# Attention outputs of the second pass by two levels of seven products, with weight sums prepared in the first pass

## The chip, the cores and the metric

The kernel runs on one core of one Trainium2 chip. The metric is the device time of one execution in microseconds. The engines are called as in the profile: PE is TensorE (PEld its weight loads), DVE is VectorE, ACT is ScalarE, POOL is GpSimd, and SP issues nearly all the DMA transfers.

## What is computed

The reference is a block of four layers over x (8 sequences of 256 rows, 1024 wide, fp32): an autocorrelation layer with a context, a linear layer with low-rank experts, an attention over the context, and a linear layer with a Fourier-transformed update. Each is added to x with a gate. The change touches the third, whose reference is, cut down:

```python
q = rope(query @ wq)            # 32 heads of 128
k, v = rope(key @ wk), value @ wv   # 8 heads; 4 query heads share one
p = softmax(mask(q @ k.T))
out = concat_heads(p @ v) @ wo  # (256 x 4096) @ (4096 x 1024)
x = x + tanh(g_xattn[1]) * out
```

Everything is fp32.

## The kernel before

**Passes and blocks.** The eight sequences are done in two passes (`p` = 0, 1) of four. A pass keeps its rows of x in SBUF (`xt`, eight tiles of 128 rows) and runs the four layers one after the other: `autocorrelation` with `keys_values` beside it, `lora_ffn`, `attention`, `fourier_ffn`. Within attention there are 16 steps `(blk, g)`: two blocks of 512 rows, and for each the eight groups of four query heads that share a key head.

**Seven products instead of eight.** Matrix products are done by one level of the Strassen-Winograd scheme: both operands are cut into 2 x 2 quarters, seven products of sums of quarters are made, in the order `SEVEN = (1, 2, 6, 7, 4, 5, 3)`, and their results are added up on eviction from PSUM. `left_operands` and `right_operands` (lines 203 and 212) make the operands with four additions each. `combine` (220) adds the products of queries, keys and values; `add_product` (252) adds those of the outputs into x, with the gate. The operand sums of wq and wo are made once, in the first block of the first pass, written to DRAM (`wq_d`, `wo_d`) and loaded from there later (`load_wq` 862, `load_wo` 884); a step loads seven tiles of 512 KB of each.

**What a step puts on the engines.** `queries` (921) makes the queries of the next step, 7 products of 8 matmuls of 128x256, evicted by VectorE and ScalarE, and rotated by `rope` (714): three VectorE multiplications and one GpSimd addition. `scores` (969) does four matmuls of 128x256 for each pair of heads, into two PSUM tiles; VectorE copies them under the mask into tiles that GpSimd has filled with a large negative number (985), and a softmax by VectorE and ScalarE follows. `values` (1006) transposes the weights on TensorE and multiplies them by v. `outputs` (942) multiplies the attention of the step before by wo: 7 products, each for two tiles of 128 rows, with two matmuls of 128x512 for a tile.

**The order** is written out by hand with generators. Each step has four quarters `i`, one for each `(n, l)`: scores, then `q_fill[i]` query products, then output products by `o_fill[i]`, in the midst of the `values` of the quarter before. The Tile framework issues the instructions of each engine from that order, as operands and buffers come free in its own planning. PSUM tiles: four of `ps_mm` (queries and outputs), two of `ps_sc` (scores), two of `ps_wa` (transposed weights and values). In SBUF the big tiles are in three groups of seven of 4 KB a partition: the tags a and b hold weights, "xn" holds operands of x.

Of the kernel before, what the change touches and what calls it, by code (L numbers as in the profile page):

```python
# [11 lines left out]
F32 = mybir.dt.float32  # L12
# [7 lines left out]
P = 128  # L20
# [26 lines left out]
def flamingo_kernel(ctx: ExitStack, tc: tile.TileContext, a: dict, out: bass.AP):  # L47
# [25 lines left out]

    tab = const.tile([P, 2, S], F32, name="tab")
    tab_q = const.tile([P, 2, S], F32, name="tab_q")
# [3 lines left out]
    def load_constants():  # L79
        nc.sync.dma_start(tab, a["rope"])  # L80
        nc.sync.dma_start(tab_q, a["rope_q"])
        nc.sync.dma_start(rows, a["rows"])
        nc.sync.dma_start(gates[:, :, 0], a["g_xattn"].partition_broadcast(P))
        nc.sync.dma_start(gates[:, :, 1], a["g_ffn"].partition_broadcast(P))
        nc.scalar.activation(tg, gates, AF.Tanh)
        nc.vector.tensor_scalar(ntg, tg, -1.0, None, ALU.mult)
        nc.sync.dma_start(gate_b, a["gate_b"].partition_broadcast(P))
# [12 lines left out]
        [dram.tile([P, 2, HALF], F32, name=f"wo_d{g}_{i}") for i in range(4)] for g in range(N_KV)  # L100
    ]

    wk_d, wv_d = (
# [115 lines left out]

    def combine(r, ps, tiles, new, dest):  # L220


        if r == 1:
            tiles["u"] = new("u")
            nc.scalar.copy(tiles["u"], ps)
        elif r == 2:
            c = dest()
            nc.vector.tensor_add(c, ps, tiles["u"])
            return c, (0, 0)
        elif r == 6:  # L230
            nc.vector.tensor_add(tiles["u"], ps, tiles["u"])
        elif r == 7:
            tiles["w"] = new("w")
            nc.vector.tensor_add(tiles["w"], ps, tiles["u"])
        elif r == 5:
            m = new("m")
            nc.scalar.copy(m, ps)
            nc.gpsimd.tensor_add(tiles["u"], tiles["u"], m)
            c = dest()
            nc.gpsimd.tensor_add(c, tiles["w"], m)  # L240
            return c, (1, 1)
        elif r == 3:
            c = dest()
            nc.vector.tensor_add(c, ps, tiles["u"])
            return c, (0, 1)
        elif r == 4:
            c = dest()
            nc.vector.tensor_sub(c, tiles["w"], ps)
            return c, (1, 0)
        return None  # L250
# [462 lines left out]

    def rope(dst, ps, cos, sin, pool):

        H = P // 2
        t0 = pool.tile([P, 2, S], F32, tag="rope0", name="rope0", bufs=1)
        t1 = pool.tile([P, 2, S], F32, tag="rope1", name="rope1", bufs=1)
        tab = lambda t: t.unsqueeze(1).to_broadcast([t.shape[0], 2, S])
        nc.vector.tensor_mul(t0, ps, tab(cos))  # L720
        nc.vector.tensor_mul(t1[0:H], ps[H:P], tab(sin[H:P, :]))
        nc.vector.tensor_mul(t1[H:P], ps[0:H], tab(sin[0:H, :]))  # L722
        nc.gpsimd.tensor_add(dst, t0, t1)  # L723

    def keys_values(n, groups, pools):

# [60 lines left out]
        for u in range(4):  # L787
# [4 lines left out]
            for r in SEVEN:  # L792
# [14 lines left out]
                out_tile = lambda: w2.tile([P, 2, S], F32, tag="kv", name=kind[1])  # L807
                dest = (lambda: new("c")) if kind == "wk" else out_tile
                done = combine(r, ps, tiles, new, dest)
                if done:  # L810
                    c, (i, j) = done
                    if kind == "wk":
                        kT = out_tile()
                        rope(kT, c, tab[:, 0, :], tab[:, 1, :], w1)
                        place = kT_d.rearrange("(q l i) p t -> q i p l t", l=2, i=2)
                        nc.sync.dma_start(
                            place[i_u, i, :, :, t0 + j * S : t0 + (j + 1) * S], kT
                        )
# [11 lines left out]

    def query_operands(xt, norm, pool, ps_t, tag):

# [3 lines left out]
        for t in range(NBT):  # L836
            xn = pool.tile([P, D], F32, tag="xn", name="xl")
            normed(xn, xt[t], mv, rstd, t)
# [6 lines left out]
        s = [big_tile("xn", [KH, S], f"xn_t{i}") for i in (1, 2, 4)]  # L845
        return right_operands(nc.vector, q, *s)

    def attention(p, xt, gq, go, keep, norms, xops):
        with (
# [6 lines left out]
            steps = [(blk, g) for blk in range(TT // NBT) for g in range(N_KV)]  # L859
            wq, wo, kv = {}, {}, {}  # L860

            def load_wq(step):
# [21 lines left out]
            def load_wo(step):  # L884
# [12 lines left out]
                else:  # L897
                    ops = {}
                    where = {1: a["wo"][g, 0, 0], 2: a["wo"][g, 1, 0], 3: a["wo"][g, 1, 1]}
                    where |= dict(zip((5, 7, 6, 4), wo_d[g]))  # L900
                    for r in SEVEN:
                        ops[r] = big_tile(go, [2, HALF], f"wo_{r}")
                        nc.sync.dma_start(ops[r], where[r])
                wo[step] = ops

            def load_kv(step):
                blk, g = step
                r0 = p * BP * S + blk * NB
                kT = w2.tile([P, NB], F32, tag="kv", name="kT", bufs=4)
                nc.sync.dma_start(kT, kT_d[g, :, r0 : r0 + NB])  # L910
                v = w2.tile([P, NBT, DH], F32, tag="kv", name="v", bufs=4)
                nc.sync.dma_start(
# [8 lines left out]
            def queries(step, qT):  # L921
# [3 lines left out]
                for r in SEVEN:  # L925
                    ps = ps_mm.tile([P, 2, S], F32, tag="mm", name="ps_q")
                    for l in range(2):
                        for c in range(KH):
# [6 lines left out]
                            )  # L935
                    done = combine(r, ps, tiles, lambda tag: half(tag, 1), lambda: half("c", 2))
                    if done:
                        qT[done[1]] = half("qT", 8)
                        rope(qT[done[1]], done[0], tab_q[:, 0, :], tab_q[:, 1, :], w1)
                    yield  # L940

            def outputs(step, ops):
# [11 lines left out]
                for r in SEVEN:  # L954
                    for t in range(2):
# [9 lines left out]
                        flat = [y.rearrange("p b s -> p (b s)") for y in part[t]]  # L965
                        add_product(r, po, x[t], tg_x[1], ntg_x[1], flat)
                    yield

# [37 lines left out]
            def values(step, l, n, got, oT, fill):  # L1006
# [14 lines left out]
                for i in range(2):  # L1021
                    for c in range(2):
# [6 lines left out]
                        )  # L1029
                oT[n][l] = half("oT", 8)  # L1030
                nc.scalar.copy(oT[n][l], av)

            def fill_from(gen, n):
                for _ in range(n):
                    next(gen, None)

            load_wq(steps[0])
            load_kv(steps[0])
# [4 lines left out]
            load_wq(steps[1])  # L1043
            last, before, nothing = None, None, iter(())

            q_fill = {0: (2, 2, 1, 1), len(steps) - 1: (0, 0, 0, 0)}
            o_fill = {len(steps) - 1: (2, 2, 2, 1)}
            oT = [[None, None], [None, None]]
            for k, step in enumerate(steps):
# [7 lines left out]
                else:  # L1057
                    q_gen = nothing
                o_gen = nothing
                for i, (n, l) in enumerate(((0, 0), (0, 1), (1, 0), (1, 1))):  # L1060
                    got = scores(step, l, n, qT)
                    nq = q_fill.get(k, (3, 3, 1, 0))[i]
                    no = o_fill.get(k, (0, 1, 3, 3))[i]
                    fill_from(q_gen, nq)
                    if i > 0:
                        fill_from(o_gen, no - 1)
                    if before is not None:
                        values(*before, lambda: fill_from(o_gen, 1 if no else 0))
                    before = step, l, n, got, oT
                    if i == 0 and k > 0:  # L1070
                        s = [half(f"oS{j}", 1) for j in (1, 2, 4)]
                        o_gen = outputs(last[0], left_operands(nc.gpsimd, last[1], *s))
                        fill_from(o_gen, no)
                    if i == 2 and k + 2 < len(steps):
                        if steps[k + 2][1] == 0:
                            blk = steps[k + 2][0]
                            xb = xt[blk * NBT : (blk + 1) * NBT]
                            xops[blk] = query_operands(xb, norms[blk], w1, ps_wa, "wa")
                        load_wq(steps[k + 2])
                    if i == 0:  # L1080
                        load_wo(step)
                for gen in (q_gen, o_gen):
                    for _ in gen:
                        pass
                last = step, oT
                oT = [[None, None], [None, None]]
                qT = following
            values(*before, lambda: None)
            s = [half(f"oS{j}", 1) for j in (1, 2, 4)]
            for _ in outputs(last[0], left_operands(nc.gpsimd, last[1], *s)):  # L1090
                pass
# [66 lines left out]
    for p in range(NPASS):  # L1158
        ga, gb = ("a", "b") if p % 2 == 0 else ("b", "a")
        xt = [xpool.tile([P, D], F32, tag="x", name="x") for t in range(TT)]  # L1160
        with (
# [9 lines left out]
        ):  # L1171

            def beside():
                for n in range(p * BP * S // NB, (p + 1) * BP * S // NB):
                    yield from keys_values(n, (ga, gb), (kw1, kw2, ps_kv))
                if p == 0:
# [7 lines left out]
            steps = beside()  # L1184
            next(steps)
            if p == 0:
                load_constants()
# [10 lines left out]
        with tc.tile_pool(name="at_keep", bufs=1, reuse_waits="tile") as kp:  # L1198
            keep, norms, xops = [], {}, {}

            def before_attention(pool, ps_t, tag):
                norms[0] = norm_stats(xt[:NBT])
                xops[0] = query_operands(xt[:NBT], norms[0], pool, ps_t, tag)
                for b in range(BP):
# [158 lines left out]
```

## Time and profile before

| | us |
|---|---|
| median of three runs | 3399.09 |
| lowest, highest | 3385.71, 3401.55 |
| profiled execution | 3396.83 |
| its span | 3395.0 |

The profile's stages, by windows of the trace (us from the start of the span; busy time of each engine in the stretch):

| stretch | stage | PE | DVE | POOL | GB/s |
|---|---|---|---|---|---|
| 0 to 440 | first pass, autocorrelation, keys and values | 394.85 | 327.10 | 210.31 | 178 |
| 440 to 600 | first pass, first linear layer | 159.79 | 101.31 | 33.66 | 120 |
| 600 to 1640 | first pass, attention | 1031.78 | 732.23 | 438.31 | 125 |
| 1640 to 2090 | last layer, then the second pass's first layer | 431.61 | 299.92 | 202.74 | 141 |
| 2090 to 2226 | second pass, first linear layer | 136.00 | 68.55 | 22.84 | 60 |
| 3283 to 3395 | second pass, last layer | 105.00 | 50.59 | 24.89 | 38 |

The stretch that is missing here, 2226 to 3283, is the second pass's attention; the prediction shows it. In such a line each engine has its busy time and, in brackets, the number of its instructions; at the end stand the granted clock of TensorE, the busy share of the DMA engines and what they moved in GB/s. A line of the timeline has the start, the time from the first start to the last end of a run of like instructions, the engine, the source line, the operation, its tiles and how many there are. Matmul records overlap, so the rate is read from start to start.

### The profile page before, as it was taken

Reading aid. Unit: us, or ns where it says so; the run is one execution under the profiler, and the core shown is the slowest. Engines: PE = TensorE matmul, PEld = TensorE weight load, DVE = VectorE, ACT = ScalarE, POOL = GpSimd, SP = SyncE. Lnnn points to the kernel's source line nnn. Section 1 sums busy time; section 2 is a strip of 40 time slices with the busy share of each in tenths; the row PEclk is TensorE's granted clock in tenths of the full one; section 3 lists DMA queues with packets and bytes.
Section 4 is the critical chain, followed back from the end, with each engine's and each line's share of the span. In section 5 each row is a group of like instructions: output and inputs, shape, how many; then the busy total and the mean of one; then the engine's idle time right before and its main releaser. Section 6 shows DMA issues by size and latency. Waiting matters only on the chain. (4 is left out here: it accounts for less than half of the span.)

```text
span 3395.0 us, 36926 instructions
## 1 busy us (share of the span) xinstructions
PE 3314.1 (98%) x12784; PEld 2279.1 (67%) x12784; DVE 2252.4 (66%) x4229; ACT 859.7 (25%) x2061; POOL 1354.6 (40%) x1213
## 2 busy tenths in 40 slices
PE   8899999999999999999999999999999999999999
PEld 6566546767767776775467766577767776776654
DVE  7787666877777666665657775556666666666563
ACT  1233111322222222222123321112222322222220
POOL 4665212344443443344335542123443444344332
PEclk9999999999999999999999999999999999999999
DMA  7433634333333333343153424053333333333411
GB/s 270 170 115 102 207 115 155 130 140 127 137 127 131 121 119 123 118 155 118 56 196 130 147 96 146 17 173 115 118 125 120 115 118 121 121 118 122 158 44 50
DMA packets 161864, 431.72 MB, mean 127 GB/s; under 512 B 21476, under 2 KB 56292, under 8 KB 161678
## 3 DMA queue, kind: packets, MB, share of 16 engines
q1 hardware_dynamic: 160526, 425.17, 36.3%
q0 software_dynamic: 1152, 4.19, 0.3%
q8 instruction: 102, 1.67, 0.2%
q14 instruction: 84, 0.69, 0.1%
HBM read 350.66 MB, written 78.64 MB: 126 GB/s over the span
## 5 line engine op out<-in xcount | busy, mean ns | idle before, releaser
L723 POOL TENSOR_TENSOR qT<-rope,rope 128x512 f32<-128x512 f32 x128 | 170.2, 1330 | 867.5 <-DVE rope L722 867.5
L958 PE MATMUL po<-wo,oT 128*128 128x512 f32 x960 | 432.1, 593 | 0.0
L929 PE MATMUL ps_q<-xn,wq 128*128 128x256 f32 x1920 | 428.9, 379 | 0.0
L375 DVE SCALAR_TENSOR_TENSOR x<-po,tg,x 128x512 f32<-128x512 f32 x376 | 269.1, 745 | 196.0 <-PE po L958 70.5
L929 PEld LDWEIGHTS ps_q<-xn,wq 128*128 128x128 f32 x1920 | 364.8, 190 | 50.5 <-PE po L682 0.5
L991 ACT ACTIVATE s<-s,nmx 128x256 f32<-128x256 f32 x512 | 256.0, 501 | 277.0 <-DVE nmx L988 276.5
L986 DVE COPY_PREDICATED s<-keep,ps_s 128x512 f32<-128x512 uint8 x256 | 185.9, 729 | 182.2 <-PE ps_s L977 177.7
L958 PEld LDWEIGHTS po<-wo,oT 128*128 128x128 f32 x960 | 177.4, 190 | 175.6 <-issue 170.5
L958 PE MATMUL po<-wo,oS 128*128 128x512 f32 x640 | 287.7, 592 | 0.3 <-DVE x L375 0.3
L929 PE MATMUL ps_q<-xn_t,wq 128*128 128x256 f32 x1280 | 285.6, 379 | 0.0
L1018 ACT COPY wT<-pt 128x512 f32<-128x512 f32 x256 | 138.1, 590 | 515.9 <-PE pt L1012 515.7
L929 PEld LDWEIGHTS ps_q<-xn_t,wq 128*128 128x128 f32 x1280 | 243.2, 190 | 33.1
L1023 PE MATMUL av<-wT,v 128*128 128x256 f32 x1024 | 246.2, 383 | 5.1 <-ACT wT L1018 5.1
L977 PE MATMUL ps_s<-kT,qT 128*128 128x256 f32 x1024 | 247.9, 379 | 0.0
L1023 PEld LDWEIGHTS av<-wT,v 128*128 128x128 f32 x1024 | 191.4, 190 | 80.0 <-issue 44.0
L1000 DVE TENSOR_SCALAR s<-s,tot 128x256 f32<-128x256 f32 x512 | 220.0, 470 | 7.7
L985 POOL MEMSET s<- 128x512 f32 x256 | 130.0, 527 | 220.7 <-PE pt L1012 219.0
L958 PEld LDWEIGHTS po<-wo,oS 128*128 128x128 f32 x640 | 118.9, 190 | 136.7 <-issue 128.9
L977 PEld LDWEIGHTS ps_s<-kT,qT 128*128 128x128 f32 x1024 | 191.6, 190 | 25.3 <-DVE x L375 0.5
L258 POOL TENSOR_TENSOR x<-x,part 128x512 f32<-128x512 f32 x80 | 109.1, 1364 | 229.5 <-ACT part L257 222.1
L988 DVE TENSOR_REDUCE nmx<-s 128x2 f32<-128x512 f32 x256 | 175.0, 685 | 8.3
L263 POOL TENSOR_TENSOR x<-x,part 128x512 f32<-128x512 f32 x80 | 104.7, 1310 | 172.7 <-DVE part L375 157.0
(257 smaller groups left out, 5594.0 us busy)
## 6 DMA issues: line engine op xcount, KB each, us to landing
wq<-in_wq_dram SPq DMA_DIRECT2D x104, 512.0 KB, 3.2
wo<-in_wo_dram SPq DMA_DIRECT2D x104, 512.0 KB, 3.2
wq<-wq_d SPq DMA_DIRECT2D x96, 512.0 KB, 3.2
wo<-wo_d SPq DMA_DIRECT2D x96, 512.0 KB, 3.2
w<-w_d SPq DMA_DIRECT2D x36, 512.0 KB, 4.8
wk<-in_wk_dram SPq DMA_DIRECT2D x26, 512.0 KB, 5.9
wv<-in_wv_dram SPq DMA_DIRECT2D x26, 512.0 KB, 3.8
wk<-wk_d SPq DMA_DIRECT2D x24, 512.0 KB, 4.5
```

Of the source, the lines that this page charges most:

```text
L375: nc.vector.scalar_tensor_tensor(xs, ps, g, xs, ALU.mult, ALU.add)
L723: nc.gpsimd.tensor_add(dst, t0, t1)
L929: nc.tensor.matmul(ps[:, l, :], wops[r][:, l, c, :], xo[r][:, c, :], start=(c == 0), stop=(c == KH - 1),)
L958: nc.tensor.matmul(po, ops[r][:, h, t * P : (t + 1) * P], wops[r][:, h, :], start=(h == 0), stop=(h == 1),)
L977: nc.tensor.matmul(ps[:, t, :], qT[i, n][:, l, t * P : (t + 1) * P], kT[:, n * S : (n + 1) * S], start=True, stop=True,)
L985: nc.gpsimd.memset(s, MASKED)
L986: nc.vector.copy_predicated(s, keep[b], ps)
L988: nc.vector.tensor_reduce(nmx, s, AX.X, ALU.max, negate=True)
L991: nc.scalar.activation(s[:, t, :], s[:, t, :], AF.Exp, bias=nmx[:, t : t + 1], accum_out=tot[:, t : t + 1],)
L1000: nc.vector.tensor_scalar(s[:, t, :], s[:, t, :], tot[:, t : t + 1], None, ALU.mult)
L1018: nc.scalar.copy(wT[i], pt)
L1023: nc.tensor.matmul(av[:, i, :], kv[step][1][:, n * 2 + c, :], wT[i][:, c, :], start=(c == 0), stop=(c == 1),)
```

## The change

In the second pass the outputs of two steps (groups g and g+1 of one block) are multiplied together, as a product of 512 x 1024 by 1024 x 1024, by two levels of the scheme. The outer level has seven products as before, and each of those is again seven products of 128 x 256 by 256 x 256: 49 products of two matmuls of 128x256 for two steps, where there were 28 of two matmuls of 128x512. `outputs_of_two` issues them one at a time. The operands of the inner level on the side of the attention are made by GpSimd while the outer product before runs. VectorE adds the seven inner products up from PSUM, with the gate, into the 128x512 tiles `co`; VectorE and GpSimd add these into x.

The weights for the inner level are sums of the stored wo operands. `finer_weights` makes them on GpSimd in the first pass, in 28 portions, two in each step from the third on, and writes them to DRAM (`wo2_d`); `stream_wo` loads them in the second pass, seven tiles ahead, in place of `load_wo`.

Further parts: in the second pass query product 5 is added by VectorE alone (`alone`), without the copy by ScalarE and two additions by GpSimd; `rope` works in place with one scratch tile in place of two, and the tile `c` is gone; the buffers of kT and v go from 4 to 3, of qT from 8 to 7, and those of oT from 8 to 13 in the second pass; the table `tab` lies in a pool of the first stage and is loaded in each pass; the normalized rows for the second block's queries lie in the group "xn", not in a tile of their own.

```diff
-    def rope(dst, ps, cos, sin, pool):
+    def rope(x, cos, sin, pool):
...
-        nc.vector.tensor_mul(t0, ps, tab(cos))
-        nc.vector.tensor_mul(t1[0:H], ps[H:P], tab(sin[H:P, :]))
-        nc.vector.tensor_mul(t1[H:P], ps[0:H], tab(sin[0:H, :]))
-        nc.gpsimd.tensor_add(dst, t0, t1)
+        nc.vector.tensor_mul(t[0:H], x[H:P], tab(sin[H:P, :]))
+        nc.vector.tensor_mul(t[H:P], x[0:H], tab(sin[0:H, :]))
+        nc.vector.tensor_mul(x, x, tab(cos))
+        nc.gpsimd.tensor_add(x, x, t)
...
+        elif r == 5 and alone:
+            c = dest()
+            nc.vector.tensor_add(c, ps, tiles["w"])
+            nc.vector.tensor_add(tiles["u"], ps, tiles["u"])
+            return c, (1, 1)
...
+            def finer_weights():
+                for two in range(N_KV // 2):
+                    for n, r in enumerate(SEVEN):
...
+                        for k in range(2):
+                            nc.sync.dma_start(w[k], wo_operand(two * 2 + k, r))
...
+                        nc.gpsimd.tensor_sub(t45[:, 1], q[0][1], q[0][0])
+                        nc.gpsimd.tensor_sub(t67[:, 1], q[1][1], q[0][1])
+                        nc.gpsimd.tensor_sub(t67[:, 0], q[1][1], t45[:, 1])
+                        nc.gpsimd.tensor_sub(t45[:, 0], t67[:, 0], q[1][0])
+                        nc.sync.dma_start(wo2_d[two][:, n, 0], t67)
+                        nc.sync.dma_start(wo2_d[two][:, n, 1], t45)
+                        yield
...
+                for n, src in enumerate(places):
+                    for coming in places[len(tiles) : n + 7]:
+                        tiles.append(big_tile(go, [2, 2, S], "wo"))
...
-                kT = w2.tile([P, NB], F32, tag="kv", name="kT", bufs=4)
+                kT = w2.tile([P, NB], F32, tag="kv", name="kT", bufs=3)
...
+            def outputs_of_two(blk, qs):
...
+                s1 = [half("oT", 13) for _ in qs]
+                for q, s in zip(qs, s1):
+                    nc.gpsimd.tensor_add(s, q[1][0], q[1][1])
+                    nc.gpsimd.tensor_sub(q[1][0], q[0][0], q[1][0])
...
+                        for i, (op, y, z) in {
+                            5: (nc.gpsimd.tensor_add, q[1][0], q[1][1]),
+                            7: (nc.gpsimd.tensor_sub, q[0][0], q[1][0]),
+                            6: (nc.gpsimd.tensor_sub, 5, q[0][0]),
+                            3: (nc.gpsimd.tensor_sub, q[0][1], 6),
+                        }.items():
+                            made[i] = w2.tile([P, 2, P], F32, tag="oI", name=f"oI{i}", bufs=8)
...
+                    for r2 in SEVEN:
+                        w = next(wo_stream)
+                        po = ps_mm.tile([P, S], F32, tag="mm", name="po")
+                        for h in range(2):
+                            nc.tensor.matmul(
+                                po, left[r2][:, h, :], w[:, h, :], start=(h == 0), stop=(h == 1)
+                            )
+                        scaled = nc.vector.scalar_tensor_tensor
+                        if r2 == 1:
+                            u = quarter("o_u", 1)
+                            nc.scalar.activation(u, po, AF.Copy, scale=g1)
+                        elif r2 == 2:
+                            scaled(c[0][:, 0, :], po, g1, u, ALU.mult, ALU.add)
+                        elif r2 == 6:
+                            scaled(u, po, g1, u, ALU.mult, ALU.add)
+                        elif r2 == 7:
+                            v = quarter("o_w", 1)
+                            scaled(v, po, g1, u, ALU.mult, ALU.add)
+                        elif r2 == 4:
+                            scaled(c[1][:, 0, :], po, g2, v, ALU.mult, ALU.add)
+                        elif r2 == 5:
+                            scaled(c[1][:, 1, :], po, g1, v, ALU.mult, ALU.add)
+                            scaled(u, po, g1, u, ALU.mult, ALU.add)
+                        elif r2 == 3:
+                            scaled(c[0][:, 1, :], po, g1, u, ALU.mult, ALU.add)
+                        if r2 in (1, 2, 6, 7):
+                            next(coming[1], None)
+                        if r2 != 3:
+                            yield
...
+                        if r == 1:
+                            add(nc.gpsimd, x[t][0][0])
+                        elif r == 2:
+                            add(nc.vector, x[t][0][0])
+                        elif r == 6:
+                            add(nc.vector, part[t])
+                            nc.gpsimd.tensor_add(x[t][0][1], x[t][0][1], part[t])
+                        elif r == 7:
+                            nc.vector.tensor_add(ct, ct, part[t])
+                            add(nc.gpsimd, x[t][1][0])
+                            add(nc.gpsimd, x[t][1][1])
...
+            if paired:
+                q_fill = {0: (2, 2, 1, 1), 1: (2, 2, 2, 1), end: (0, 0, 0, 0)}
+                o_fill = {k: (0, 5, 10, 10) if k % 2 == 0 else (3, 5, 8, 8) for k in range(end)}
+                o_fill[end] = (6, 6, 6, 6)
...
+                    if k > 1 and i % 2 == 0:
+                        next(fine, None)
```

## The prediction

> **What bounds the kernel now.** I read the page's busy shares first, then the table of windows with edges at the stages, then two steps of the second pass's attention by windows, groups and waits, and last TensorE's timeline there.
>
> ```profile
> PE 3314.1 (98%) x12784; PEld 2279.1 (67%) x12784; DVE 2252.4 (66%) x4229; ACT 859.7 (25%) x2061; POOL 1354.6 (40%) x1213
> ...
> 2226.00:3283.00 1057.00, 1055.12 (x4258) 759.70 (x4256) 672.73 (x1169) 293.14 (x781) 421.84 (x412) 1.00 0.36 121
> ...
> 2475.17:2606.47 131.30, 131.30 (x529) 94.61 (x528) 82.25 (x143) 35.67 (x96) 52.98 (x53) 1.00 0.35 120
> ```
>
> The second line is the second pass's attention: TensorE is busy for 1055 of 1057 us at clock 1.00. The third is two of its sixteen steps (65.65 us each): TensorE 131.3 of 131.3 us, VectorE 82, GpSimd 53. A busy TensorE can still hide slack, so the spacing of matmuls has to be checked:
>
> ```profile
> 3133.91 1.89 PE L977 MATMUL ps_s<-kT,qT 128*128 128x256 f32 x8
> 3135.64 3.60 PE L958 MATMUL po<-wo,oT 128*128 128x512 f32 x8
> 3139.07 3.60 PE L958 MATMUL po<-wo,oS 128*128 128x512 f32 x8
> 3142.51 1.04 PE L1012 MATMUL pt<-ident,s 128*128 128x128 f32 x8
> ...
> 3150.27 7.07 PE L929 MATMUL ps_q<-xn,wq 128*128 128x256 f32 x32
> 3157.18 3.62 PE L929 MATMUL ps_q<-xn_t,wq 128*128 128x256 f32 x16
> ```
>
> Each matmul of the code is two records. From start to start, eight records of 512 columns take 3.435 us (0.429 us each), 32 of 256 columns 6.91 us (0.216 each), and eight of 256 columns into two PSUM tiles, four records to a tile, 1.73 us (0.216). A step holds 112 records of queries, 56 of outputs, 32 each of scores and values, 32 transposes (8 in 0.87 us): 24.2 + 24.0 + 6.9 + 6.9 + 3.5 = 65.5 us, the step's whole length. So the stage is bound by the number of columns that TensorE streams, with no gap.
>
> ```profile
> PEld po L958 <- DVE x L375: 0.5, 2, 0.2
> ...
> L958 PEld LDWEIGHTS po<-wo,oT x63: 190/190/192, 2475.0 to 2602.0; 128*128 128x128 f32 x63
> ...
> 2505.34 1.28 POOL L207 TENSOR_TENSOR oT<-oT 128x512 f32<-128x512 f32 x1
> ...
> 2506.58 1.27 POOL L208 TENSOR_TENSOR oS<-oS,oT 128x512 f32<-128x512 f32 x1
> ...
> 2506.75 2.60 DVE L1000 TENSOR_SCALAR s<-s,tot 128x256 f32<-128x256 f32 x2
> ```
>
> The only wait of TensorE on an evicting engine in those 131 us is 0.5 us. A weight load (190 ns) fits under a 256-column matmul (216 ns), but not by much. The last three lines show what GpSimd does to VectorE: two scalings of 0.35 us take 2.60 us while GpSimd adds.
>
> **What the Trainium skill says.** *Perfetto Trace Analysis*, Identifying the Most-Contended Engine, says that matmul busy share is no measure of headroom; hence the spacing above. *VectorE: DVE Perf Modes*, The TRN2 errata, gives an fp32 tensor_tensor as (N+151)/0.96 ns: 691 ns at 512, and this trace has 691 (the combine of queries), so 424 ns at 256. *GPSIMD Engine Reference*, Key points, says that it shares its SBUF interfaces with VectorE, in contention with two-port modes and two-input instructions; the 2.60 us agree.
>
> **The change part by part** (second pass first; a pair is two steps, eight pairs).
>
> *TensorE.* Removed per pair: 112 records of 512 columns, 112 x 0.4294 = 48.1 us. Added: 49 products of two matmuls, 196 records of 256 columns, 196 x 0.2158 = 42.3 us; the shape is that of a scores tile, measured dense at 0.216. Gain 5.8 us a pair, 46 us in all. Queries, scores, values and transposes stay.
>
> *VectorE.* Removed per pair: 28 evictions (16 + 4 + 4 + 4 in the groups), 11.5 + 3.0 + 3.0 + 3.0 = 20.5 us. Added: 49 evictions of 128x256 by scalar_tensor_tensor (seven for each outer product, one more on ScalarE). No row has this form. From below 0.424 (the page's figure), from above 0.745 - 256/0.96 = 0.478 (the 512 row less its elements); I take 0.46: 22.5 us. Eight outer adds of 128x512 at 0.69: 5.5. The query product 5 goes from ScalarE and GpSimd to two VectorE adds: 4 x 0.69 = 2.8. VectorE goes from 82 to 92.5 us, in a pair that shrinks to 125.5: 74%. It stays below TensorE on the average.
>
> *GpSimd.* Removed: 8 sums (10.2), 16 adds to x (20.8, with 1.27 to 1.35 each), 4 adds of product 5 (5.0). Added: 8 sums of whole tiles (10.2), 28 of 128x256, and 14 outer adds (17.8). The 256 form is not in the trace: half of 1.27 from below; from above the slope to that guide page's 4497 ns at 2048 elements (Elementwise section), (4497-1267)/1536 = 2.1 ns an element, so 0.73: I take 0.73, 20.4 us. From 53 to about 65 of 125.5 us.
>
> *Buffers.* A product now fills its PSUM tile in 0.86 us, not 1.72, and there are still four tiles (ps_mm, shared with queries): TensorE can run 3.4 us ahead of eviction where it had 6.9. A softmax chain on VectorE (two copies 0.73, two reductions 0.69, four scalings 0.35 to 0.47, two reciprocals) is about 4.5 to 5 us. In the last two quarters of an even step 20 products are put: TensorE 20 x 0.863, two sets of scores, values and transposes (4.3 each), one query product 3.45: 29.4 us; VectorE two chains 9.9, 20 products at 0.46 + 0.11 for outer adds 11.4, a query combine and one or two rotations 3 to 5.3: 24.3 to 26.6 us, 83 to 91%. The same quarters before: 32.7 against 22 to 24, about 70%, with no stall. Behind a late eviction stand the next products, and behind those on TensorE's queue the transposes that feed the values. From below nothing (a later eviction can't gain), from above 1 us in each of 32 such quarters; I take 0.3: 10 us.
>
> *Weights.* Loads go from 14 tiles of 512 KB a pair to 12.25 MB in 28 tiles, 7 ahead. DMA moves 120 GB/s at a share of 0.36 here; 5.4 MB more in 125 us add about 44 GB/s. Seven tiles are 14 products, 12 us, against 3.2 us to landing. On SP, these loads wait on TensorE in turn with the query loads, which are a step ahead. Nothing.
>
> *Edges.* The second step loses its outputs as filler: the first step, already so before, had one wait of 0.92 us; 1 us. The tail after the last values has 42 us of products instead of 21; GpSimd needs (20.4 + 17.8 + 5.1)/7 = 6.2 us for each outer product against 6.04 of TensorE: 1 us, and the first sums 2 us: 3 us.
>
> *First pass.* 28 portions of weight sums, two a step over fourteen steps: each issues two loads, four GpSimd subtractions (5.1 us, 142 in all) and two stores, 2 MB, some 64 GB/s more. GpSimd has 53 of 131 us there too. Behind a portion on GpSimd stand the memsets of s and the rotations' adds; the scores' eviction waits for the former. Behind its stores on SP stand the loads of wq and wo, refilled a step ahead. GpSimd's and DMA's idle time cover it; if the cover failed, TensorE would pay up to one chain of 5.1 + 3.2 us a portion. From 0 (added work can't gain) to 8; I take 0.1 each: 3 us. More GpSimd time also slows VectorE, which has a third free.
>
> *The rest.* Rotation in place, one scratch tile, three buffers for kT and v, seven for qT, tab in a pool, x-hat in the xn group. The key tile now stays from combine to store, with two buffers: in the trace the stores at 1945.5, 1951.8 and 1961.9 lie over 6 us apart and land in 2.5 us, so a buffer is back in time. v then comes only after the scores that read the old kT, with about 20 us left. Nothing.
>
> Sum: -46 + 10 + 1 + 3 + 3 = -29 us. From the profiled execution (3396.8 us, of which 1.8 lie around its span) that is 3368. This execution lies 2.3 us under the median of the runs shown, 3399.1.
>
> **Rivals.**
> - *Full gain, 0.26:* nothing stalls but the tail, 3396.8 - 46 + 3 = 3354. For it: the dense timeline and VectorE's 74%. Against: the shorter run-ahead.
> - *Eviction takes the bound's place in the bursts, 0.18:* 0.8 us in each of 32 quarters is 26 us instead of 10: 3384. For it: 83 to 91% on VectorE, GpSimd holding up its scalings. Against: TensorE's 0.5 us of such waits now.
> - *The sums in the first pass stall the scores, 0.08:* GpSimd waits in its queue for a portion's load, the memset behind comes late, both score tiles in PSUM fill, and TensorE stops. It decides from about 2.3 us a portion (28 x 2.3 = 64 against 46 + 17 to be visibly slower). At 3 us, in place of the 0.1 above: 3368 + 81 = 3449. Against it: of the 182.2 us that VectorE's copies wait in the whole profile, 177.7 are for TensorE's scores, next to nothing for a memset.
> - *The change doesn't reduce columns as it says:* excluded by the count, 49 x 256 x 2 for 28 x 512 x 2.
>
> **How the numbers follow.** My forecast, 3368, has 0.48. About 0.5% (17 us) is what a measurement can tell from no change, so faster means below 3382. The first case and full gain are faster (0.74), and a third of the eviction case (0.06): 0.80. The rest of it is within 0.5% (0.12), the stalled sums are slower (0.08). The range runs from 3348 (full gain with a tail at nothing, 3351, and the 0.1% by which executions differ) to 3392 (eviction at its upper bound, 32 us, which is 3390, and the same again).
>
> **What would show it.** In the second pass's attention, records of the output products at 0.216 us spacing and pairs of steps near 126 us prove the column count; a pair of 130 or more, with TensorE's weight loads waiting on VectorE, proves the eviction case. The 128x256 eviction should show 0.42 to 0.48 us. In the first pass steps should stay at 65.65 us; 68 or more, with VectorE's copies waiting on GpSimd's memset, proves the stalled sums. I am wrong in kind if the second pass's attention keeps its 1057 us, or the stage ahead of it grows.

## The result, and the profile after

| | before | after |
|---|---|---|
| median, us | 3400.32 (3385.71 to 3405.47) | 3423.82 (3419.21 to 3428.41) |
| span of the profiled execution, us | 3395.0 | 3417.4 |

The changed kernel is slower: its time is 1.0078 times that of before, with an interval from 1.0048 to 1.0107. The forecast was 3368 and the range ended at 3392. The head of the page after, whose first line answers to the first that the prediction shows of before (its transfers were 431.72 MB, 127 GB/s):

```profile
PE 3286.5 (96%) x13456; PEld 2409.7 (71%) x13456; DVE 2401.6 (70%) x4493; ACT 855.2 (25%) x2069; POOL 1625.4 (48%) x1501
...
DMA packets 223849, 534.95 MB, mean 157 GB/s; under 512 B 25972, under 2 KB 103796, under 8 KB 223646
```

TensorE is busy for 27.6 us less (3314.1 before) in a span that is 22.4 us longer. So some 50 us in which it stands came in, more than was saved. To find where, I cut both traces at four marks: the first query matmul and the end of the outputs in each pass's attention.

| stage, us | before | after | difference |
|---|---|---|---|
| start to the first pass's attention | 562.7 | 556.6 | -6.1 |
| first pass, attention | 1060.3 | 1110.7 | +50.4 |
| between the attentions | 603.4 | 611.7 | +8.3 |
| second pass, attention | 1056.1 | 1024.7 | -31.4 |
| to the end | 112.5 | 113.7 | +1.2 |

The second pass's attention gained what was forecast. The first pass's attention, where the change only adds the weight sums, lost more than that. The windows after, the whole second attention and two of its steps (busy time of PE, PEld, DVE, ACT, POOL, with the number of instructions; then the granted clock, the DMA share and GB/s):

```profile
2279.00:3304.00 1025.00, 1013.23 (x4929) 885.85 (x4927) 760.43 (x1429) 289.07 (x789) 546.37 (x588) 1.00 0.52 168
2527.20:2654.70 127.50, 126.10 (x613) 110.39 (x613) 94.16 (x176) 35.20 (x97) 68.38 (x75) 1.00 0.52 167
```

A pair of steps takes 127.5 us where it took 131.3. VectorE has 94.2 us in it and GpSimd 68.4. Two steps of the first pass's attention, the same place before and after:

```profile
684.00:815.00 131.00, 131.00 (x528) 94.50 (x528) 100.87 (x159) 35.66 (x96) 56.91 (x53) 1.00 0.38 137
```

```profile
714.00:856.00 142.00, 134.22 (x528) 95.12 (x527) 114.59 (x159) 35.14 (x97) 92.35 (x81) 0.98 0.64 230
```

Two things are to be read here. VectorE was at 101 of 131 us in this place already before the change, not at 82 as in the window that the prediction showed of the second pass: in the first block of the first pass it also makes the operand sums of wq and wo, about 16 additions of 1.2 us in two steps. And with the portions on GpSimd (92 us for 57), VectorE's own time grows to 115 us although it has the same 159 instructions. One form of instruction shows it best, the scaling of the softmax (count | busy us, mean ns of one | idle us before it), before and after in these windows:

```profile
L1000 DVE TENSOR_SCALAR s<-s,tot 128x256 f32<-128x256 f32 x32 | 14.0, 473 | 0.5
```

```profile
L1163 DVE TENSOR_SCALAR s<-s,tot 128x256 f32<-128x256 f32 x32 | 23.6, 772 | 0.5
```

What TensorE waits for, in the first pass's attention of before (first lines) and from 556 to 1250 us of after (second lines; the longest are shown): us in total, times, longest.

```profile
PE av L1023 <- ACT wT L1018: 4.2, 2, 2.5
PE pt L843 <- DVE xl L360: 0.4, 1, 0.4
PE po L958 <- DVE x L375: 0.3, 1, 0.3
```

```profile
PE po L1013 <- DVE qT L250: 24.4, 6, 6.5
PE po L1013 <- DVE x L381: 8.0, 5, 6.3
PE av L1186 <- ACT wT L1181: 4.4, 2, 2.4
```

In the whole stage TensorE stands 34 us longer than before (39 for 5), and the same 4258 records keep it busy 16 us longer (1072.0 for 1056.0), of which the last section says more. The output products wait for a PSUM tile that VectorE has not yet emptied: the four tiles `ps_mm` are shared by queries and outputs, L250 is the last eviction of a query product, L381 the eviction of an output. The timeline after shows how one of these waits comes about:

```profile
725.94 2.13 POOL L932 TENSOR_TENSOR fine_t<-fine_t,fine 128x512 f32<-128x512 f32 x1
...
733.05 1.26 POOL L246 TENSOR_TENSOR qT<-w,m 128x512 f32<-128x512 f32 x1
734.18 3.60 PE L1013 MATMUL po<-wo,oT 128*128 128x512 f32 x8
734.26 0.97 POOL L1148 MEMSET s<- 128x512 f32 x2
734.34 0.69 DVE L725 TENSOR_TENSOR rope<-qT,tab_q 64x512 f32<-64x512 f32 x1 [2.38 <-POOL qT L246]
...
740.26 2.38 DVE L1163 TENSOR_SCALAR s<-s,tot 128x256 f32<-128x256 f32 x2
...
742.74 2.50 DVE L1163 TENSOR_SCALAR s<-s,tot 128x256 f32<-128x256 f32 x2
...
745.16 0.68 DVE L250 TENSOR_TENSOR qT<-ps_q,u 128x512 f32<-128x512 f32 x1
...
745.89 3.78 PE L1013 MATMUL po<-wo_t,oS 128*128 128x512 f32 x4 [6.41 <-DVE qT L250]
```

GpSimd finishes a portion at 728, then makes a rotation's addition and only after it those of query product 5, so VectorE idles 2.38 us for one of them; from 734 it works without a gap, but its four scalings take 4.9 us in place of 1.4 (0.35 us each is their median), while GpSimd is adding the next portion; the eviction L250 comes at 745.2, and TensorE has stood for 6.41 us.

GpSimd's idle time ahead of the portions' subtractions, and what ended it (us, times):

```profile
  DMA wo_d<-fine_t: 52.9, 12
  DMA fine<-wo_d: 35.9, 9
  DMA fine<-in_wo_dram: 18.6, 4
```

GpSimd stood 107 us in its queue until the portions' own stores and loads had landed. The portions do not come two a step: the trace has their first subtractions at 709, 721, 739, 755, 770, 783 and 796, then a pause to 851. They lie in runs of 3, 7, 7, 7 and 4 with pauses between, about 14 us from one portion to the next within a run, all 28 before 1195 us, nearly all in the block in which VectorE is fullest. Seven is the number of portions of one pair of groups. The loss goes with how much of them falls into one step. From the first query product of a step to that of the next, and from the third step on, the steps with 19 to 27 of the subtractions took 72.1 to 84.9 us, the two with seven 67.0 and 68.4, those with one or none 65.6 or 65.7 (before: 65.7, and 70.4 at the change of the block, where after has its 84.9).

### The profile page after: what moved, and what is told of

It is laid out like the page before. It is cut to its first block, busy times and chain, and to the rows that moved or that the text cites. A ratio compares the mean times of both kernels' runs of the same rounds, so it can differ in the third digit from the quotient of the medians.

```text
span 3417.4 us, 39838 instructions
## 1 busy us (share of the span) xinstructions
PE 3286.5 (96%) x13456; PEld 2409.7 (71%) x13456; DVE 2401.6 (70%) x4493; ACT 855.2 (25%) x2069; POOL 1625.4 (48%) x1501
## 5 line engine op out<-in xcount | busy, mean ns | idle before, releaser
L728 POOL TENSOR_TENSOR qT<-qT,rope 128x512 f32<-128x512 f32 x128 | 169.1, 1321 | 591.0 <-DVE qT L727 591.0
L381 DVE SCALAR_TENSOR_TENSOR x<-po,tg,x 128x512 f32<-128x512 f32 x248 | 178.5, 744 | 135.7 <-PE po L688 42.5
L1163 DVE TENSOR_SCALAR s<-s,tot 128x256 f32<-128x256 f32 x512 | 262.5, 553 | 7.5
L1076 PE MATMUL po<-wo,oI 128*128 128x256 f32 x896 | 217.0, 382 | 9.4 <-POOL oI L1059 8.3
L1013 PE MATMUL po<-wo,oT 128*128 128x512 f32 x448 | 201.8, 593 | 1.0 <-DVE x L381 1.0
L1076 PEld LDWEIGHTS po<-wo,oI 128*128 128x128 f32 x896 | 167.4, 190 | 38.2 <-POOL oI L1059 11.8
L264 POOL TENSOR_TENSOR x<-x,part 128x512 f32<-128x512 f32 x48 | 65.3, 1361 | 221.1 <-ACT part L263 221.1
L1076 PE MATMUL po<-wo,oT 128*128 128x256 f32 x672 | 167.6, 379 | 2.0 <-DVE co L1091 2.0
L1194 ACT COPY oT<-av 128x512 f32<-128x512 f32 x128 | 74.9, 585 | 369.8 <-PE av L1186 369.8
```

What stands on the lines that cost most here:

```text
L381: nc.vector.scalar_tensor_tensor(xs, ps, g, xs, ALU.mult, ALU.add)
L728: nc.gpsimd.tensor_add(x, x, t)
L1013: nc.tensor.matmul(po, ops[r][:, h, t * P : (t + 1) * P], wops[r][:, h, :], start=(h == 0), stop=(h == 1),)
L1076: nc.tensor.matmul(po, left[r2][:, h, :], w[:, h, :], start=(h == 0), stop=(h == 1))
L1163: nc.vector.tensor_scalar(s[:, t, :], s[:, t, :], tot[:, t : t + 1], None, ALU.mult)
```

## The experiments

Two readings were to be told apart. *Load*: GpSimd's additions lengthen VectorE's instructions, and where VectorE has already 101 of 131 us this makes its evictions late. *Queue*: GpSimd waits in its queue for a portion's transfers, and what stands behind is late. Stage times, in us (the ratios of the runs are to executions of before made beside them, median 3402.72 or 3400.99 us):

| run | first attention | second | median | ratio |
|---|---|---|---|---|
| before | 1060.3 | 1056.1 | | |
| after | 1110.7 | 1024.7 | 3423.82 | 1.0078 (1.0048 to 1.0107) |
| no_sums | 1058.9 | 1025.0 | 3366.55 | 0.9897 (0.9881 to 0.9914) |
| moves_only | 1061.0 | 1024.0 | 3369.04 | 0.9908 (0.9892 to 0.9925) |
| spread | 1072.8 | 1024.6 | 3383.93 | 0.9949 (0.9933 to 0.9966) |
| late | 1060.9 | 1023.8 | 3369.90 | 0.9904 (0.9887 to 0.9920) |
| sums_only | 1113.4 | 1024.6 | 3420.49 | 1.0049 (1.0032 to 1.0066) |
| light | 1103.7 | 1023.8 | 3410.75 | 1.0025 (1.0015 to 1.0034) |
| alone_both | 1100.8 | 1026.3 | 3409.09 | 1.0029 (1.0018 to 1.0041) |
| late_vec | 1060.9 | 1026.7 | 3367.75 | 0.9894 (0.9878 to 0.9911) |
| dense_first | 1104.1 | 1024.7 | 3413.93 | 1.0038 (1.0026 to 1.0051) |
| dense_light | 1058.2 | 1026.4 | 3366.10 | 0.9895 (0.9878 to 0.9911) |

**No sums at all (no_sums).** The second pass loads other stored weights in their place, as many bytes.

```diff
-                        d = wo2_d[g // 2][:, n]
...
+                        d = [wo_d[g + k][0].rearrange("p k (j s) -> p k j s", s=S) for k in range(2)]
...
-            fine = finer_weights() if p == 0 else nothing
+            fine = nothing
```

> Leaves out the weight sums of the first pass (the second pass loads stored sums of the outer level in their place, as many bytes). Three theories of the 50 us that the first pass's attention has gained (1110.7 us against 1060.3). Sums theory: GpSimd's subtractions come in bursts in the first block and hold up VectorE and the query product 3. Transfer theory: the 2 MB that each portion moves and its waits on SP and GpSimd's queue. Buffers theory: rotation in place and the smaller buffers. Sums and transfers: first pass's attention back at 1060 us, within 5; whole about 3374. Buffers: it stays near 1110, whole 3424. The second pass's attention should stay at 1024 us in all of them.

The first attention is back at 1058.9 us and the second keeps its 1025.0. The whole loss lies in the portions; the second pass by itself is a gain of 1%.

**Transfers without sums (moves_only).** The portions load and store as before, what they store is what they loaded.

```diff
-                        nc.gpsimd.tensor_sub(t45[:, 1], q[0][1], q[0][0])
...
-                        nc.sync.dma_start(wo2_d[two][:, n, 0], t67)
-                        nc.sync.dma_start(wo2_d[two][:, n, 1], t45)
+                        for k in range(2):
+                            part = w[k].rearrange("p k (j s) -> p k j s", s=S)
+                            nc.sync.dma_start(wo2_d[two][:, n, k], part)
```

> Leaves out the four GpSimd subtractions of each portion; the loads are stored back as they are, so that all transfers stay. Sums theory: first pass's attention at 1060 to 1070 us, whole 3374 to 3385. Transfer theory: 1095 to 1110, whole 3410 to 3424. Both in part: between.

1061.0 us: 2 MB more a portion through SP's queue and the DMA engines, 186 GB/s over the stage where it was 131, cost nothing by themselves here. What costs has to do with GpSimd.

**Two portions a step, as the code reads (spread).** `issue_after` keeps the four subtractions of a portion behind the quarter's memset in the plan of GpSimd's queue, so that they can't be drawn ahead in bursts.

```diff
-                    nc.gpsimd.memset(s, MASKED)
+                    pin[0] = nc.gpsimd.memset(s, MASKED)
...
+                        with tc.issue_after(pin[0].ins):
+                            nc.gpsimd.tensor_sub(t45[:, 1], q[0][1], q[0][0])
...
```

> All the work of the changed kernel, with the subtractions of each portion queued on GpSimd behind the fill of that quarter's s tile, so that two portions fall on each of the steps 3 to 16. Sums theory (it is the bursts in the first block): first pass's attention at 1065 to 1080 us, whole 3380 to 3393. If each portion costs the same wherever it is: 1105 to 1115, whole 3420. Transfer theory: the same bytes at half the rate, 1080 to 1100.

1072.8 us: three quarters of the loss go, and the same work is now faster than before. The steps in the midst of the first block take 67.8 us (65.7 before), those of the second 65.7, with the same two portions each. So where a portion lies, and how many lie together, decides what it costs.

**All of it in the second block (late).** As spread, one portion in each quarter, from the second block on.

```diff
-                    if k > 1 and i % 2 == 0:
+                    if k >= N_KV:
                         next(fine, None)
```

> All the work, with one portion in each quarter of the second block of the first pass alone, where VectorE makes no weight sums for wq and wo. Sums theory with VectorE's load as its condition: first pass's attention at 1060 to 1070 us although the portions come as densely as in the bursts, whole 3374 to 3385. If dense portions cost wherever they are, or by transfers: 1090 to 1110, whole 3405 to 3424.

1060.9 us, and 3369.90 in all, 0.9904 (0.9887 to 0.9920) of before: the loss is gone and the gain is whole. Two steps of it, and its scalings:

```profile
1109.00:1242.00 133.00, 131.65 (x529) 94.26 (x528) 100.78 (x156) 38.31 (x99) 94.43 (x85) 1.00 0.70 245
```

```profile
L1165 DVE TENSOR_SCALAR s<-s,tot 128x256 f32<-128x256 f32 x32 | 25.9, 851 | 0.5
```

GpSimd is as full as after the change (94 us) and slows the scalings even more (851 ns). But VectorE begins here at 87 us, as this place in no_sums shows, and ends at 101, which two steps can carry:

```profile
1109.00:1240.00 131.00, 131.00 (x528) 94.51 (x527) 87.01 (x156) 38.30 (x99) 52.57 (x53) 1.00 0.38 120
```

**Sums without transfers, dense in the first block (sums_only).** As late, but from the third step on, and from one pair of tiles that is loaded once; nothing is stored, and the second pass loads other weights, as in no_sums.

```diff
+                w = [w1.tile([P, 2, HALF], F32, name=f"fine{k}") for k in range(2)]
...
-                            nc.sync.dma_start(w[k], wo_operand(two * 2 + k, r))
...
-                        nc.sync.dma_start(wo2_d[two][:, n, 0], t67)
-                        nc.sync.dma_start(wo2_d[two][:, n, 1], t45)
...
-                    if k > 1 and i % 2 == 0:
+                    if k > 1:
```

> Leaves out the portions' transfers: the four GpSimd subtractions run on two tiles loaded once, one portion in each quarter from the third step to the ninth, all in the first block and about as dense as in the changed kernel; the second pass loads other stored sums. Contention theory (GpSimd's adds lengthen VectorE's instructions, VectorE has no room in this block): first pass's attention at 1085 to 1115 us, scalings of s at 700 ns or more in those steps. Queue theory (GpSimd stands waiting for a portion's load with the rotations' adds and the memsets behind it): 1060 to 1070 us.

1113.4 us, and GpSimd stands for no transfer ahead of any of these subtractions: the subtractions alone are enough for the whole loss, if they lie in the first block.

**VectorE relieved (light).** The changed kernel without VectorE's operand sums of wq and wo; raw quarters stand in their place.

```diff
-                    s = [big_tile(gq, [2, KH, DH], f"wq_s{i}") for i in (1, 2, 4)]
-                    ops = left_operands(nc.vector, q, *s)
+                    ops = {1: q[0][0], 2: q[0][1], 3: q[0][1], 4: q[1][1], 5: q[1][0], 6: q[0][0], 7: q[1][0]}
...
-                    s = [big_tile(go, [2, HALF], f"wo_t{i}") for i in (1, 2, 4)]
-                    ops = right_operands(nc.vector, q, *s)
+                    ops = {1: q[0][0], 2: q[1][0], 3: q[1][1], 4: q[1][0], 5: q[0][1], 6: q[0][0], 7: q[0][1]}
```

> Leaves out VectorE's operand sums for wq and wo in the first block (raw tiles are used and stored in their place); the portions stay as they are, in bursts, with all transfers. Contention theory, with VectorE's load as its condition: VectorE has 21 us more room in two steps, first pass's attention at 1058 to 1070 us. If GpSimd's own queue or the transfers decide: 1090 to 1110 us.

A miss for the load reading: VectorE is down to 96 us in two steps, and the stage still takes 1103.7. The waits of two steps (us in total, times, longest):

```profile
DVE s L1147 <- POOL s L1146: 11.4, 3, 8.1
POOL fine_t L927 <- DMA fine<-in_wo_dram: 10.4, 1, 10.4
DVE rope L725 <- POOL qT L246: 9.6, 2, 5.3
...
POOL fine_t L927 <- DMA fine<-wo_d: 7.2, 1, 7.2
```

GpSimd stands up to 10.4 us for the load of a portion, and VectorE stands for GpSimd's memset and its additions of product 5. So in the unfixed placement what lies behind a portion in GpSimd's queue is late. But standing for a transfer is only a part of it. TensorE waits 21.3 us for the eviction L250 here, in six waits, and in the 20 us before five of the six GpSimd stood for no transfer longer than 1.9 us (7.0 us before the sixth; two waits for another query eviction, 5.0 us in all, came after 10.4 and 8.1 us). One of the five:

```profile
797.12 1.60 POOL L930 TENSOR_TENSOR fine_t<-fine_t,fine 128x512 f32<-128x512 f32 x1
...
801.59 1.27 POOL L246 TENSOR_TENSOR qT<-w,m 128x512 f32<-128x512 f32 x1
...
802.89 0.69 DVE L725 TENSOR_TENSOR rope<-qT,tab_q 64x512 f32<-64x512 f32 x1 [5.30 <-POOL qT L246]
...
813.66 2.80 PE L1011 MATMUL po<-wo,oS 128*128 128x512 f32 x3 [2.90 <-DVE qT L250]
```

The four subtractions of a portion, from 792.4 to 798.7 without a pause, are enough to make the addition L246 late; VectorE idles 5.30 us for it, and its eviction L250, on which TensorE then waits, falls behind.

**Product 5 without GpSimd in the first pass too (alone_both).**

```diff
-                    done = combine(r, ps, tiles, new, dest, paired)
+                    done = combine(r, ps, tiles, new, dest, True)
```

> All the work; query product 5 is added by VectorE alone in the first pass too, so that product 3, behind which TensorE waits, no longer depends on two adds in GpSimd's queue. If it is GpSimd's queue that makes product 3 late: first pass's attention at 1065 to 1090 us. If it is VectorE's load: the two adds of 0.69 us a step make it no better, 1105 to 1120 us.

1100.8 us, 10 less than after. It takes one of the things that stand behind a portion off GpSimd's queue and puts two additions more on VectorE. The time lies between the two ranges expected, and does not decide between the readings.

**Dense in the first block, all work, fixed (dense_first); the same with VectorE relieved (dense_light).** The first is late with `if k > 1` in place of `if k >= N_KV`; the second has light's edit as well.

> All work of the changed kernel; the portions are fixed behind a quarter's memset, one in each quarter from the third step on, so six of the seven steps lie in the first block, where VectorE also makes the operand sums of wq and wo. It is the version with the sums in the second block, moved to the first, nothing else. Theory A (the sums cost where VectorE has 101 of 131 us already, because GpSimd's adds slow it down): about 8 us in each of the six steps, first pass's attention near 1112 us, scalings of 128x256 at 0.9 us or more, no waits of GpSimd for a portion's load over 3 us; whole about 3420. Theory B (what costs is GpSimd standing in its queue for a portion's transfers, which only the unfixed placement brings): near 1065 us, whole about 3373.

> As the version fixed in the first block, but VectorE's operand sums of wq and wo in the first block are left out (the stored operands are raw quarters, so what is computed from them is another sum). VectorE has then about 20 us less in two steps. Theory A (VectorE's load is the condition): the cost goes, first pass's attention 1058 to 1072 us, scalings still at 0.8 us or more. Theory B (GpSimd's standing in its queue is the condition, VectorE's load is not): the same time as the version fixed in the first block, within 8 us.

1104.1 and 1058.2 us. The edits of this pair differ in one thing, VectorE's operand sums, and it makes 46 us. Their windows:

```profile
782.00:926.00 144.00, 136.02 (x532) 96.36 (x531) 117.06 (x159) 35.52 (x96) 101.68 (x85) 0.98 0.67 241
```

```profile
769.00:901.00 132.00, 130.89 (x527) 93.93 (x526) 95.11 (x142) 35.67 (x96) 94.08 (x85) 1.00 0.75 263
```

And TensorE's waits up to 1250 us, of dense_first and of dense_light:

```profile
PE po L1015 <- DVE x L381: 16.9, 7, 5.0
PE po L1015 <- DVE qT L250: 13.2, 5, 3.7
```

```profile
PE po L1013 <- DVE x L381: 2.0, 2, 1.1
```

VectorE at 117 us can't keep up, at 95 it can, though GpSimd has the same portions and the scalings are as long (878 ns in dense_light). The expectation that dense_first shows no wait of GpSimd over 3 us for a load did not hold everywhere: there were four waits for a load from `wo_d`, 18.2 us in all, outside this window. dense_light has none; but sums_only has none either and loses as much as dense_first, so the loss doesn't need them.

The placements together, first attention in us:

| | VectorE makes the operand sums | left out |
|---|---|---|
| portions drawn ahead in bursts | 1110.7 | 1103.7 |
| fixed, one a quarter, first block | 1104.1 | 1058.2 |
| fixed, one a quarter, second block | 1060.9 | |

Where the portions are fixed, VectorE's load is the condition: that is shown. Where they are drawn ahead in bursts, relieving VectorE is not enough, and GpSimd's queue makes its followers late; light shows it. How much of that is standing for transfers (113.4 us ahead of the portions' subtractions in light, 0.2 in dense_light, for anything), and how much the order and the density of the portions, stays open: fixing changes all three at once (a portion some 14 us after another in a run, some 17 when fixed), and they were not varied apart. In after itself standing came before few of the waits: in the 20 us before each of its five longer waits for L250, GpSimd stood for a transfer 1.2 us at most.

**A better kernel than late? (late_vec).** The second pass's remaining waits of TensorE are for GpSimd. Two of the 14 additions into x that GpSimd makes for a pair of steps go to VectorE.

```diff
                         if r == 1:
-                            add(nc.gpsimd, x[t][0][0])
+                            add(nc.vector, x[t][0][0])
```

> All the work, portions in the second block as in the run named late, and in the second pass the outer adds of product 1 to x by VectorE instead of GpSimd, since an add of this kind stood in GpSimd's queue before the inner operand that TensorE waited for (1.13 us a pair). If that add is the cause: second pass's attention at 1013 to 1018 us instead of 1024, whole 3360 to 3366. If the wait only moves, or VectorE's 1.4 us more a pair tell: 1022 to 1030, whole 3368 to 3374.

The second range came: the second attention takes 1026.7 us (1023.8 in late), and the whole is equal to late within the intervals. TensorE's wait for GpSimd did go, and others took its place; late (first line) and late_vec:

```profile
PE po L1078 <- POOL oI L1061: 8.4, 12, 1.2
```

```profile
PE po L1078 <- issue: 3.6, 6, 0.6
PE po L1078 <- DVE co L1098: 2.9, 7, 0.4
PE po L1078 <- POOL oI L1061: 1.6, 6, 0.3
```

So the moved additions were part of what TensorE waited for, but taking them away only moved the wait.

## Why the prediction was wrong

- **TensorE's columns in the second pass: right.** Forecast -46 + 10 + 1 + 3 = -32 us, edges and tail included; measured -31.4, and -29.4 to -32.3 in the ten runs. The pair was put at 125.5 us plus the evictions, and took 127.5. VectorE was put at 92.5 and had 94.2; GpSimd at 65 and had 68.4. Four of the new records take 0.86 us from start to start, which is the 0.216 us a record that was taken:

```profile
2589.66 1.03 PE L1076 MATMUL po<-wo,oT 128*128 128x256 f32 x4
2590.52 1.89 PE L1076 MATMUL po<-wo,oI 128*128 128x256 f32 x8
```

- **The 10 us of late evictions: about the size, by luck; the place was wrong in the main.** They were to be late evictions by VectorE. The waits of TensorE in that stage are:

```profile
PE po L1076 <- POOL oI L1059: 8.3, 12, 1.1
PE po L1076 <- DVE co L1091: 2.0, 1, 2.0
PE po L1076 <- DVE o_u L1094: 1.1, 1, 1.1
```

  Of 11.4 us, 8.3 are for the inner operands that GpSimd makes, which the forecast priced as a wait in the tail alone; 3.1 are for VectorE.
- **The unknown forms.** The eviction of 128x256 was taken at 0.46 us between 0.424 and 0.478, GpSimd's addition of 128x256 at 0.73 (0.746 measured):

```profile
L1084 DVE SCALAR_TENSOR_TENSOR co<-po,tg,o_u 128x256 f32<-128x256 f32 x6 | 2.9, 476 | 1.1 <-ACT o_u L1082 1.1
...
L1059 POOL TENSOR_TENSOR oI<-oT 128x256 f32<-128x256 f32 x14 | 10.2, 746 | 2.3 <-PE po L1076 2.1
```

  The upper bound, worked out from the 512 row of this kernel, was the right one (0.476 measured); the lower, 0.424, from the Trainium skill, *VectorE: DVE Perf Modes*, The TRN2 errata, which is for tensor_tensor, does not hold for this form with a PSUM operand.
- **The failed step: "First pass".** It took 0.1 us a portion, 3 us in all. It was 50.4 / 28 = 1.8 us a portion. Three sentences of it were wrong. "28 portions of weight sums, two a step over fourteen steps": they came in bursts of up to seven, nearly all in the first block. "GpSimd's and DMA's idle time cover it": GpSimd's idle time was there, but not at the moment when what stands behind a portion falls due. "More GpSimd time also slows VectorE, which has a third free": a third fits the mean over the first pass's attention (732 of 1040 us busy) or two steps of the second pass (82 of 131); in the first block VectorE has 101 of 131 us, 23% free, before its instructions are lengthened. The Trainium skill, *GPSIMD Engine Reference*, Key points, names this contention, the prediction quoted it and saw 2.60 us for two scalings, and still put no term for it in the sum. What the runs showed in its place: these additions alone, with no transfer, cost the first attention 53 us where VectorE is full (sums_only), and 0.6 us where it is not (late, which has the transfers too).
- **The rival of the stalled sums: right in kind, partly in mechanism.** It asked for 2.3 us a portion to be slower, set against the full gain; against the gain of 31 us that came, 1.8 was enough. Steps of 68 us or more came, as it said. The memset is late (VectorE waits 19.9 us for it up to 1250 us of the trace after), but TensorE hardly stops on the score tiles (1.0 us); it stops on those that queries and outputs share. And sums_only shows the loss with no transfer to wait for, where the rival asked for a wait for a load.
- **The rest at nothing.** Rotation in place, fewer buffers of kT and qT, the table: no_sums has all of these, and its first attention is within 1.4 us of before. The +8.3 us between the attentions and the -6.1 ahead are not explained: in the ten runs, whose edits lie in the attentions, they take 603.5 to 610.4 and 555.8 to 562.4 us.

## What to carry to other kernels

Work that is moved to an idle engine has to be priced in the stretch where it will lie: read every engine's window there, not that of a stage that looks alike. Where a framework plans the order, a position in the code is not a position in the queue; the trace, or a constraint as in late, says where the work lies. An addition on GpSimd beside a full VectorE is work for VectorE too.

## What the runs showed of the hardware

- GpSimd's additions cost VectorE time: in late 112 of them (some 142 us) raised VectorE's busy time in the first attention from 744.2 us (no_sums) to 786.3, 0.3 us for each us of GpSimd. It falls mostly on a few forms: the scaling of 128x256, 0.35 us at the median, has a mean over two steps of 0.47 before and of 0.64 (spread) to 0.91 (dense_first) beside the portions, while the copies under the mask (0.73 us before and after) and the reductions (0.69) are as long as they were. The first line is of no_sums, the second of late:

```profile
560.00:1620.00 1060.00, 1055.34 (x4258) 760.93 (x4257) 744.24 (x1228) 292.60 (x781) 439.58 (x420) 1.00 0.40 131
```

```profile
561.00:1622.00 1061.00, 1055.06 (x4256) 759.16 (x4254) 786.32 (x1228) 292.59 (x781) 585.68 (x529) 1.00 0.54 186
```

- These 42 us more on VectorE, and 55 GB/s more of transfers, leave the stage's length where it was: TensorE is at 1055 us of 1060 and of 1061.
- In the trace of after, TensorE's granted clock falls to half at the end of a long wait and stays there for some microseconds of work. Two windows of after, before and from 743.8 us, about the wait of 6.41 us that ended at 745.9:

```profile
736.00:743.80 7.80, 3.49 (x9) 1.23 (x7) 7.66 (x10) 2.19 (x8) 7.12 (x6) 1.00 0.16 49
743.80:750.60 6.80, 4.71 (x10) 2.52 (x11) 6.72 (x10) 0.00 (x0) 2.01 (x2) 0.50 0.80 248
```

  The first attention of after has seven such stretches of 3.4 or 6.8 us, 34 us in all, one at each of TensorE's seven waits of 2.0 us or more; those of before and of late have none, though before has one wait of 2.5 us, so the length of the wait alone does not decide it. Work of 34 us at half the clock would take up to 17 us more (an estimate from these stretches), about the 16 us of longer busy time: a stall costs more than its own length.
